# Row maxima of the attention scores by way of DRAM, two groups ahead, and another order of DVE work and loads in the first slot

## The chip, the cores and the metric

The kernel runs on one core of a Trainium2 chip. The metric is the device time of one launch in microseconds, the median of three runs. The engines are TensorE (PE; PEld is its weight load), VectorE (DVE), ScalarE (ACT), GpSimd (POOL) and SyncE (SP), whose queue starts nearly all transfers. Everything is float32.

## The reference

One pre-norm transformer layer, cut to what matters. There are 4 batches of 512 tokens, width 512, 32 query heads and 8 key heads of 16 dimensions, so 4 query heads share a key head; the feed-forward width is 1376.

```
x = resid                                   # (4, 512, 512)
n = layernorm(x)
q, k = rope(n @ Wq), rope(n @ Wk);  v = n @ Wv
att   = (q . k) / 4, causal                 # per query head, 512 x 512
probs = softmax(att)                        # needs the maximum of each row, or a bound of it
x = x + (probs @ v) @ Wo
n = layernorm(x)
x = x + (silu(n @ W_gate.T) * (n @ W_up.T)) @ W_down.T
```

## The kernel before, in words

The attention of a batch is worked in 8 groups of 4 heads. The 32 groups (`GROUPS`) are numbered through: group g belongs to batch g // 8. Four heads of a group stand in the four 32-row quarters of the partitions, and PE works with 32 rows at a time.

For each group the scores are made twice. The plain scores (`scores`, L436: queries on partitions, keys along the row) are only there to find the maximum of each row. `greatest` reads them: ACT copies heads 2 and 3 out of PSUM (L447), and DVE runs one masked minimum of the negated scores for each head and query tile (L454), first on heads 0 and 1 straight from PSUM, then on the copy. The negative maxima go to columns of the tile `low`. They are then needed along a row, not down a column: `lowered` has PE transpose the four 128 x 128 pieces of `low` (L471), and DVE adds the result to `qa` (L472). `qa` is the masked copy of a group's queries (`masked`, on POOL); in each quarter it has a row that `masked` leaves zero, and there the negative maxima come to stand. The keys carry a one at that place. So the second pass (`lowered_scores`, L480: keys on partitions, queries along the row) gives scores with the maximum already subtracted; ACT takes the exponential (L487), POOL clears the half above the diagonal (L491), and `averages` (L509) multiplies with the values. Their quotients are made later, from the queues `later` and `later_act`.

The four PSUM banks `sc` (two `pairs`) serve both passes in turn, for three rounds of query tiles (`rounds`), so each round of one pass waits until the round of the other has been read.

The order is written out by hand. `slot(b, steps)` runs the 8 groups of batch b. While it makes the lowered scores of group g, it makes the plain scores and maxima of group g + 1. Between these it places pieces of other matmul work: `gap` takes from `steps` what the shares in `shares` allow. Slot 0 gives the projections of batches 1 to 3; slots 1 to 3 give the output projection and the feed-forward of the batch before, and after slot 3 the last batch's follow alone. DVE work that may wait, such as the layer norms, stands in the queue `aside` and is taken by `do(aside)`.

A projection is made in two halves of matmuls (`halved`); its `finish` follows at once. For queries and keys that is `rotated`: DVE shuffles (L228) and multiplies (L230), POOL does the rest. `transposed` turns a normalised tile on PE (L195) and copies it out, the odd tiles on DVE (L198) and the even on ACT (L200). All of them take one of three PSUM banks from `bank`.

Weight loads (`load_w`, L158) and x loads stand on SP in the order of the program. Before slot 0 the kernel loads x of batch 0, all of wk, rope, wq, wv and wo, normalises and projects batch 0, and makes the plain scores of group 0; the norms and transposes of batch 1 are spread between its three rounds. Feed-forward weights are loaded by `load_f` two column blocks ahead.

Of the kernel before, what the change touches and what calls it, by code (L numbers as in the profile page):

```python
# [47 lines left out]
SWAP = [(d + 16) % 32 for d in range(32)]  # L48

# [25 lines left out]
def preln_block_kernel(  # L75
# [56 lines left out]


# [25 lines left out]

    def bank():  # L160
        return ps_mm.tile([P, T], F32, tag="mm", name="mm")
# [30 lines left out]
    def transposed(xn, i, xnT):  # L192
# [4 lines left out]
        if i % 2:  # L197
            nc.vector.tensor_copy(xnT[:, :, ts(i, P)], src)  # L198
        else:
            nc.scalar.copy(xnT[:, :, ts(i, P)], src)  # L200

    def halved(products, finish):
# [8 lines left out]
        def two():  # L211
            for step in products[len(products) // 2 :]:
                step(made["ps"])
            finish(made["ps"])
# [200 lines left out]
    def masked(g):  # L415
# [4 lines left out]
        qa[g] = work.tile([P, T], F32, tag="qa", name="qa", bufs=2)  # L420
# [19 lines left out]
    def greatest(g, at, lo, hi):  # L440
# [4 lines left out]
        hf = GROUPS[g][2]  # L445
        copy = work.tile([P, 2, T], F32, tag="copy", name="copy", bufs=2)
        nc.scalar.copy(copy[:, :, lo:hi], pairs[1][:, :, lo:hi])  # L447
        for pair, src in enumerate((pairs[0], copy)):
            for i, c in at:
                n = P * (i + 1)  # L450
                for r in range(2):
                    junk = work.tile([P, T], F32, tag="junk", name="junk")
                    row = 32 * (2 * pair + r) + 16 * (1 - hf)
# [8 lines left out]
                        accum_out=low[hf][:, i, row : row + 1],  # L462
                    )

    def lowered(g):
# [6 lines left out]
        nc.vector.tensor_tensor(qa[g], qa[g], pt, ALU.add)  # L472

# [70 lines left out]

    for i in range(NT):
        load_xr(0, i)
    load_w(wk_sb, wk)
    nc.sync.dma_start(out=rope_sb, in_=rope)
    load_w(wq_sb, wq)
    load_w(wv_sb, wv)  # L550
    load_w(wo_sb, wo)
# [7 lines left out]
    for t in low:  # L559
        nc.gpsimd.memset(t, 0.0)  # L560
    for n in range(4):
        nc.gpsimd.memset(values(n), 1.0)
    for cost, step in turned:
        step()
    begin1[1]()
    for cost, step in start[:4]:
# [6 lines left out]
    scores(0, rounds[0][0])  # L573
    greatest(0, *rounds[0])
    do(aside, 3)
    for cost, step in start[6:8]:
        step()
    scores(0, rounds[1][0])
    greatest(0, *rounds[1])
    do(aside, 2)  # L580
    for cost, step in (turned1[0], *start[8:10], turned1[1]):
        step()
    scores(0, rounds[2][0])
    greatest(0, *rounds[2])
    for cost, step in (*turned1[2:], *start[10:]):
        step()
    masked(1)
    lowered(0)

# [7 lines left out]
    def slot(b, steps):  # L597

        steps = deque(steps)
        total = sum(cost for cost, _ in steps)  # L600

        shares = [0.19, 0.17, 0.19, 0.2, 0.25]
        done, part, n = 0.0, 0.0, 0

        def gap():
            nonlocal done, part, n
            part += shares[n % 5]
            n += 1
            done = fill(steps, total * part / 8, done)

        for g in range(8 * b, 8 * b + 8):
# [3 lines left out]
            probabilities(((0, 0),), e0, T)  # L615
# [107 lines left out]
```

## Time and profile before

| | us |
|---|---|
| three timed runs | 989.32, 989.39, 993.88 |
| median | 989.39 |
| the profiled execution, whole | 993.68 |
| its span, first to last instruction | 992.0 |
| mean granted TensorE clock | 0.979 |
| first lowered scores of groups 0, 8, 16, 24 start at | 52.56, 225.31, 427.3, 635.0 |
| tail after the last slot, from about | 842 |

The span is what the engines' views divide; the profiled execution's own time is 1.7 us longer. Busy times overlap between engines and do not add up. A group of instructions has its line, engine, operation, and destination<-source; in the timeline each row begins with start and duration in us, and in brackets stands the idle time before it with what ended it. An answer by windows gives for each stretch its length and, engine by engine, the busy time and the number of instructions. PE and PEld overlap.

### The profile page before, as it was taken

To read this page: it belongs to the slowest core of one execution; us is meant where nothing else is said; L and a number is where in the kernel's file an instruction comes from. 1 tells how busy PE (TensorE), PEld (TensorE's weight loads), DVE (VectorE), ACT (ScalarE), POOL (GpSimd) and SP (SyncE) were. 2 spreads that over 40 slices of the span, in tenths; PEclk is the share of its full clock that TensorE was granted. 3 is DMA by queue.
4 is the path that set the end of the run, shared out by engine and by line. 5 is a ranking of instruction groups with operands and counts; after the bars stand their busy time and mean duration, and the time that the engine had idled before them with its cause. 6 is when DMAs were issued, how large, how long until landed. Compare 5 with 4: busy or idle time off the path is not lost.

```text
span 992.0 us, 12710 instructions
## 1 busy us (share of the span) xinstructions
PE 926.5 (93%) x4800; PEld 412.3 (42%) x4800; DVE 535.8 (54%) x1488; ACT 296.6 (30%) x385; POOL 216.0 (22%) x291
## 2 busy tenths in 40 slices
PE   6779887889899999999999999999999999999998
PEld 3334343443344444444444444444444443444443
DVE  5766677767665656475555564655655553312110
ACT  0134344443334333333333433323333431010000
POOL 5353354443311111212111111111111111100000
PEclk9898899999899999999999999999999999999999
DMA  6100100000244310040112110101212102022100
GB/s 212 43 1 1 34 11 1 2 1 1 65 159 126 84 45 26 11 170 11 53 45 53 43 50 11 54 1 43 54 43 54 41 19 64 11 75 75 47 11 32
DMA packets 56813, 46.63 MB, mean 47 GB/s; under 512 B 6352, under 2 KB 48336, under 8 KB 56496
## 3 DMA queue, kind: packets, MB, share of 16 engines
q1 hardware_dynamic: 56464, 40.05, 13.9%
q10 hardware_dynamic: 288, 5.77, 1.5%
q8 instruction: 38, 0.62, 0.3%
q14 instruction: 23, 0.19, 0.1%
HBM read 38.73 MB, written 7.08 MB: 46 GB/s over the span
## 4 chain that ended last, share of the span: by engine, by line
PE 77%; DVE 10%; ACT 5%; issue 2%; POOL 1%; DVEq 0%; ACTq 0%; POOLq 0%
PE mm L375 31%; PE mm L401 15%; PE sc L480 8%; PE av L509 8%; PE sc L436 7%; DVE junk L454 6%; PE mm L327 5%; ACT e L487 5%; PE mm L471 1%; PE mm L220 1%; DVE inv L532 1%; DVE st L175 0%; PE mm L195 0%; ACT xnT L200 0%; DVE inv L528 0%
## 5 line engine op out<-in xcount | busy, mean ns | idle before, releaser
L375 PE MATMUL mm<-xnT,shared 128*128 128x512 f32 (+1 forms) x704 | 324.2, 606 | 2.5 <-ACT xnT L200 2.5
L487 ACT ACTIVATE e<-sc 128x1024 f32<-128x1024 f32 (+1 forms) x192 | 160.6, 881 | 281.0 <-PE sc L480 268.0
L454 DVE CUSTOM_DVE_ANT_0 junk<-sc,mask 128x512 f32<-128x512 f32 (+3 forms) x256 | 125.6, 490 | 130.7 <-PE sc L436 94.1
L491 POOL TENSOR_SCALAR_AFFINE_SELECT e<-e 128x512 f32<-128x512 f32 x128 | 83.9, 667 | 512.8 <-issue 240.6
L375 PEld LDWEIGHTS mm<-xnT,shared 128*128 128x128 f32 (+1 forms) x704 | 126.2, 188 | 166.5 <-issue 159.0
L401 PE MATMUL mm<-wd_sb,home 128*128 128x512 f32 (+1 forms) x352 | 158.5, 599 | 0.0
L454 DVE CUSTOM_DVE_ANT_0 junk<-copy,mask 128x512 f32<-128x512 f32 (+3 forms) x256 | 131.2, 513 | 19.7 <-DVE low L454 0.5
L447 ACT COPY copy<-sc 128x1024 f32<-128x1024 f32 (+1 forms) x96 | 83.6, 871 | 194.7 <-PE sc L436 172.0
L480 PE MATMUL sc<-qa,home 32*128 32x512 f32 (+3 forms) x1024 | 96.3, 468 | 12.4 <-DVE low L454 10.2
L436 PE MATMUL sc<-home,qa 32*128 32x512 f32 (+3 forms) x1024 | 94.3, 460 | 10.7 <-ACT e L487 10.0
L401 PEld LDWEIGHTS mm<-wd_sb,home 128*128 128x128 f32 (+1 forms) x352 | 64.9, 190 | 82.7 <-issue 81.6
L509 PE MATMUL av<-e,home 128*32 128x512 f32 (+3 forms) x1024 | 80.7, 459 | 0.0
L480 PEld LDWEIGHTS sc<-qa,home 32*128 32x128 f32 x1024 | 43.3, 184 | 81.6 <-DVE low L454 54.3
L384 DVE SCALAR_TENSOR_TENSOR g<-g,mm 128x512 f32<-128x512 f32 (+1 forms) x44 | 30.2, 686 | 86.5 <-ACT g L383 86.5
L436 PEld LDWEIGHTS sc<-home,qa 32*128 32x128 f32 x1024 | 47.2, 187 | 64.8 <-issue 21.0
L327 PE MATMUL mm<-wo_sb,cx 128*128 128x512 f32 x128 | 62.0, 623 | 5.7 <-POOL cx L533 5.7
L220 PE MATMUL mm<-xnT,shared 128*128 128x512 f32 x120 | 62.2, 655 | 1.7 <-DVE xnT L198 0.9
L386 DVE TENSOR_TENSOR home<-mm,g 128x512 f32<-128x512 f32 (+1 forms) x44 | 30.4, 690 | 52.8 <-PE mm L375 52.7
L383 ACT ACTIVATE g<-mm 128x512 f32<-128x512 f32 (+1 forms) x44 | 26.3, 598 | 100.9 <-PE mm L375 100.9
L532 DVE RECIPROCAL inv<-inv 128x256 f32<-128x256 f32 x32 | 55.3, 1739 | 0.1
L405 DVE SCALAR_TENSOR_TENSOR xr<-mm,xr 128x512 f32<-128x512 f32 x16 | 11.0, 690 | 78.7 <-PE mm L401 78.7
L509 PEld LDWEIGHTS av<-e,home 128*32 128x32 f32 x1024 | 30.0, 114 | 40.2 <-issue 37.6
(70 smaller groups left out, 561.3 us busy)
## 6 DMA issues: line engine op xcount, KB each, us to landing
shared<-in_wg SPq DMA_DIRECT2D x40, 256.0 KB, 2.8
shared<-in_wu SPq DMA_DIRECT2D x40, 256.0 KB, 2.9
xr<-in_x SPq DMA_DIRECT2D x16, 256.0 KB, 3.5
out<-xr SPq DMA_DIRECT2D x16, 256.0 KB, 2.0
xa<-in_x SPq DMA_DIRECT2D x12, 256.0 KB, 2.8
spill<-wd_sb ACTq DMA_DIRECT2D x1, 2816.0 KB, 9.0
home<-spill ACTq DMA_DIRECT2D x1, 2816.0 KB, 12.5
wd_sb<-in_wd SPq DMA_DIRECT2D x1, 2560.0 KB, 10.8
```

The costliest lines, as they stand in the source:

```text
L220: nc.tensor.matmul(ps, lhsT=w[:, k, ts(m, P)], rhs=xnT[:, k, :], start=k == 0, stop=k == NK - 1)
L327: nc.tensor.matmul(ps, lhsT=cx[m][:, ts(i, P)], rhs=wo_sb[:, m, :], start=m == 0, stop=m == 3)
L375: nc.tensor.matmul(ps[:m, :], lhsT=wgu[c][:, a, k, :m], rhs=xnTs[""][:, k, :], start=k == 0, stop=k == NK - 1)
L401: nc.tensor.matmul(py[i], lhsT=homes[n][:m, f, ts(i, P)], rhs=wd_sb[:m, f, :], start=f == 0, stop=f == NF - 1)
L436: nc.tensor.matmul(sc[r][:, c : c + n], lhsT=qa[g][rows, ts(i, P)], rhs=k[rows, :n], start=True, stop=True)
L447: nc.scalar.copy(copy[:, :, lo:hi], pairs[1][:, :, lo:hi])
L454: nc.vector.tensor_tensor_reduce(out=junk[:, :n], in0=src[:, r, c : c + n], in1=mask[:, T - n :], scale=-1.0, scalar=BIG, op0=ALU.add, op1 ...
L480: nc.tensor.matmul(sc[r][:, c : c + T - P * j], lhsT=k[rows, ts(j, P)], rhs=qa[g][rows, P * j :], start=True, stop=True)
L487: nc.scalar.activation(e[:, 2 * n : 2 * n + 2, :], pairs[n][:, :, :width], AF.Exp, scale=1.0 / math.sqrt(DH))
L491: nc.gpsimd.affine_select(out=e[:, :, c : c + P], in_=e[:, :, c : c + P], compare_op=ALU.is_ge, fill=0.0, base=0, pattern=[[0, 4], [1, P]] ...
L509: nc.tensor.matmul(av[32 * r : 32 * r + 32, P * j :], lhsT=v[:, j, 4 * (m // 2) + r, DH * (1 - hf) : DH * (3 - hf)], rhs=e[:, r, c : c + n ...
L532: nc.vector.reciprocal(r, r)
```

## The change

Three things are done.

Groups from `NEAR` = 9 on no longer use `lowered`. Their negative maxima go to a small tile `packed` (128 x 32, one column for each head and query tile). `turned_round` transposes it on DVE in blocks of 32 x 32 and stores it to DRAM (`lowest`). `laid_out` loads it from there with four transfers straight into the zero row of `qa`, each 4 x 4 pieces of 32 numbers. All five are issued on SP.

For these groups the plain scores are made two groups ahead (`h = g + 2`), `masked` runs one group earlier and `qa` has three buffers. Group 8 makes the plain scores of both group 9 and group 10, with extra gaps between them. In `gap`, shares are given by each call.

Up to the end of slot 0 (`thin`) the order differs. x of batch 1 and the first 128 columns of wq are loaded ahead of wv, the rest of wq and wo; the norms of batch 1 are made right after the first half of batch 0's key matmuls are issued, and its transposes and keys follow the third round of group 0's plain scores. Odd transposed tiles are also copied by ACT. A projection's `finish` is put off into the queue `full`, taken in `greatest` between and after the two sets of maxima (or by `bank`, if more than one is waiting). `averages(g)` stands ahead of `lowered(h)`, with a gap after it (the former also holds in later slots, where `lowered` is not called for the next group). `do(aside)` is called at other places.

```diff
@@ -130,6 +132,10 @@
     low = [const.tile([P, NT, P], F32, name=f"low{hf}") for hf in range(2)]
 
 
+    packed = [const.tile([P, 32], F32, name=f"packed{n}") for n in range(3)]
+    lowest = [dram.tile([P, 32], F32, name=f"lowest{n}") for n in range(2)]
+
+
 
     homes = [const.tile([P, NF, T], F32, name=f"home{n}") for n in range(3)] + [wd_sb]
     spill = dram.tile([P, NF, T], F32, name="spill")
@@ -157,7 +163,13 @@
     def load_w(t, src):
         nc.sync.dma_start(out=t, in_=src.rearrange("(k p) m -> p k m", p=P))
 
+
+    full = deque()
+    thin = [True]
+
     def bank():
+        while len(full) > 1:
+            full.popleft()()
         return ps_mm.tile([P, T], F32, tag="mm", name="mm")
 
 
@@ -194,7 +206,7 @@
         for k in range(NK):
             nc.tensor.transpose(pt[:, ts(k, P)], xn[:, ts(k, P)], ident)
         src = pt.rearrange("p (k q) -> p k q", k=NK)
-        if i % 2:
+        if i % 2 and not thin[0]:
             nc.vector.tensor_copy(xnT[:, :, ts(i, P)], src)
         else:
             nc.scalar.copy(xnT[:, :, ts(i, P)], src)
@@ -211,7 +223,10 @@
         def two():
             for step in products[len(products) // 2 :]:
                 step(made["ps"])
-            finish(made["ps"])
+            if thin[0]:
+                full.append(lambda: finish(made["ps"]))
+            else:
+                finish(made["ps"])
 
         return one, two
 
@@ -417,7 +432,7 @@
         if g >= len(GROUPS):
             return
         b, m, hf = GROUPS[g]
-        qa[g] = work.tile([P, T], F32, tag="qa", name="qa", bufs=2)
+        qa[g] = work.tile([P, T], F32, tag="qa", name="qa", bufs=3)
         nc.gpsimd.tensor_scalar(qa[g], homes[HOME[b]][:, m, :], halves[hf], 1.0, ALU.mult, ALU.mult)
 
     def keys_of(g):
@@ -443,14 +458,20 @@
         if g >= len(GROUPS):
             return
         hf = GROUPS[g][2]
+
+        def found(head, i):
+            if g < NEAR:
+                row = 32 * head + 16 * (1 - hf)
+                return low[hf][:, i, row : row + 1]
+            return packed[g % 3][:, NT * head + i : NT * head + i + 1]
+
         copy = work.tile([P, 2, T], F32, tag="copy", name="copy", bufs=2)
         nc.scalar.copy(copy[:, :, lo:hi], pairs[1][:, :, lo:hi])
-        for pair, src in enumerate((pairs[0], copy)):
+        def maxima(pair, src):
             for i, c in at:
                 n = P * (i + 1)
                 for r in range(2):
                     junk = work.tile([P, T], F32, tag="junk", name="junk")
-                    row = 32 * (2 * pair + r) + 16 * (1 - hf)
                     nc.vector.tensor_tensor_reduce(
                         out=junk[:, :n],
                         in0=src[:, r, c : c + n],
@@ -459,8 +480,14 @@
                         scalar=BIG,
                         op0=ALU.add,
                         op1=ALU.min,
-                        accum_out=low[hf][:, i, row : row + 1],
+                        accum_out=found(2 * pair + r, i),
                     )
+
+        maxima(0, pairs[0])
+        if lo == 0:
+            do(full, len(full))
+        maxima(1, copy)
+        do(full, len(full))
 
     def lowered(g):
 
@@ -470,6 +497,22 @@
         for i in range(NT):
             nc.tensor.transpose(pt[:, ts(i, P)], low[GROUPS[g][2]][:, i, :], ident)
         nc.vector.tensor_tensor(qa[g], qa[g], pt, ALU.add)
+
+    def turned_round(g):
+        if g >= len(GROUPS):
+            return
+        t = small.tile([P, 32], F32, tag="turned", name="turned", bufs=2)
+        nc.vector.transpose(t, packed[g % 3])
+        nc.sync.dma_start(out=lowest[g % 2], in_=t)
+
+    def laid_out(g):
+
+        if g >= len(GROUPS):
+            return
+        rows = qa[g].rearrange("(r s) (i a q) -> r s i a q", r=4, i=NT, a=4)[:, 16 * (1 - GROUPS[g][2])]
+        src = lowest[g % 2].rearrange("(a u r i) q -> u i r a q", a=4, u=2, r=4)[0]
+        for i in range(NT):
+            nc.sync.dma_start(out=rows[:, i], in_=src[i])
 
     def lowered_scores(g, at):
 
@@ -542,13 +585,14 @@
     HOME = {0: 0, 1: 1, 2: 2, 3: 1}
 
 
+    def load_columns(t, src, lo, hi):
+        nc.sync.dma_start(out=t[:, :, lo:hi], in_=src[:, lo:hi].rearrange("(k p) m -> p k m", p=P))
+
     for i in range(NT):
         load_xr(0, i)
     load_w(wk_sb, wk)
     nc.sync.dma_start(out=rope_sb, in_=rope)
-    load_w(wq_sb, wq)
-    load_w(wv_sb, wv)
-    load_w(wo_sb, wo)
+    load_columns(wq_sb, wq, 0, P)
 
     (begin1, turned1, rest1), (begin2, turned2, rest2), (begin3, turned3, rest3) = (
         projections(b, b) for b in range(1, B)
@@ -556,36 +600,38 @@
     begin, turned, start = projections(0, 0, early=True)
     begin[1]()
     do(aside, len(aside))
-    for t in low:
+    begin1[1]()
+    load_w(wv_sb, wv)
+    load_columns(wq_sb, wq, P, D)
+    load_w(wo_sb, wo)
+    for t in (*low, *packed):
         nc.gpsimd.memset(t, 0.0)
-    for n in range(4):
-        nc.gpsimd.memset(values(n), 1.0)
+    nc.gpsimd.memset(values(0), 1.0)
+    thin[0] = False
     for cost, step in turned:
         step()
-    begin1[1]()
-    for cost, step in start[:4]:
+    for cost, step in start[:1]:
+        step()
+    do(aside, len(aside))
+    for n in range(1, 4):
+        nc.gpsimd.memset(values(n), 1.0)
+    for cost, step in start[1:4]:
         step()
     masked(0)
     for cost, step in start[4:6]:
         step()
 
     rounds = (((3, 0),), 0, T), (((2, 0), (0, 3 * P)), 0, T), (((1, 2 * P),), 2 * P, T)
-    scores(0, rounds[0][0])
-    greatest(0, *rounds[0])
-    do(aside, 3)
-    for cost, step in start[6:8]:
-        step()
-    scores(0, rounds[1][0])
-    greatest(0, *rounds[1])
-    do(aside, 2)
-    for cost, step in (turned1[0], *start[8:10], turned1[1]):
-        step()
-    scores(0, rounds[2][0])
-    greatest(0, *rounds[2])
-    for cost, step in (*turned1[2:], *start[10:]):
-        step()
+    thin[0] = True
+    for at, steps in zip(rounds, ([*start[6:8]], [*start[8:10]], [*turned1, *rest1[:2]])):
+        scores(0, at[0])
+        greatest(0, *at)
+        for cost, step in steps:
+            step()
     masked(1)
     lowered(0)
+    for cost, step in start[10:]:
+        step()
 
     def fill(steps, upto, done):
         while steps and done + steps[0][0] / 2 <= upto:
@@ -598,48 +644,76 @@
 
         steps = deque(steps)
         total = sum(cost for cost, _ in steps)
-
-        shares = [0.19, 0.17, 0.19, 0.2, 0.25]
-        done, part, n = 0.0, 0.0, 0
-
-        def gap():
-            nonlocal done, part, n
-            part += shares[n % 5]
-            n += 1
-            done = fill(steps, total * part / 8, done)
-
-        for g in range(8 * b, 8 * b + 8):
+        done, part = 0.0, 0.0
+        groups = range(8 * b, 8 * b + 8)
+        shares = 8 + 0.5 * (NEAR - 1 in groups)
+        thin[0] = b == 0
+
+        def gap(share):
+            nonlocal done, part
+            part += share / shares
+            done = fill(steps, total * part, done)
+
+        for g in groups:
+            h = g + 1 if g + 1 < NEAR else g + 2
             if g % 8 == 7:
                 do(aside, len(aside))
             lowered_scores(g, ((0, 0),))
             probabilities(((0, 0),), e0, T)
+            if g + 1 > NEAR:
+                laid_out(g + 1)
             do(later)
+            if not thin[0]:
+                do(aside)
+            gap(0.17 if thin[0] else 0.19)
+            if h == NEAR + 1:
+                for at, lo, hi in rounds:
+                    scores(NEAR, at)
+                    greatest(NEAR, at, lo, hi)
+                    gap(0.17)
+                turned_round(NEAR)
+                laid_out(NEAR)
+            at, lo, hi = rounds[0]
+            scores(h, at)
+            greatest(h, at, lo, hi)
             do(aside)
-            gap()
-            at, lo, hi = rounds[0]
-            scores(g + 1, at)
-            greatest(g + 1, at, lo, hi)
-            do(aside)
-            gap()
+            gap(0.15 if thin[0] else 0.17)
             lowered_scores(g, ((1, 0), (3, 3 * P)))
             probabilities(((1, 0), (3, 3 * P)), e1, T)
             do(later_act)
             do(later)
-            do(aside)
-            gap()
+            if not thin[0]:
+                do(aside)
+            gap(0.17 if thin[0] else 0.19)
             at, lo, hi = rounds[1]
-            scores(g + 1, at)
-            greatest(g + 1, at, lo, hi)
-            gap()
+            scores(h, at)
+            greatest(h, at, lo, hi)
+            if thin[0]:
+                do(aside)
+            gap(0.17 if thin[0] else 0.2)
             at, lo, hi = rounds[2]
             lowered_scores(g, ((2, 0),))
-            scores(g + 1, at)
-            greatest(g + 1, at, lo, hi)
+            scores(h, at)
+            greatest(h, at, lo, hi)
+            if h > NEAR:
+                turned_round(h)
             probabilities(((2, 0),), e2, 2 * P)
-            masked(g + 2)
-            gap()
-            lowered(g + 1)
+            if h == NEAR - 1:
+                masked(NEAR)
+                masked(NEAR + 1)
+            elif h < NEAR:
+                masked(g + 2)
+            else:
+                masked(g + 3)
+            gap(0.17 if thin[0] else 0.25)
             averages(g)
+            if h < NEAR:
+                lowered(h)
+            if thin[0]:
+                do(aside)
+                gap(0.17)
+        thin[0] = False
+        do(full, len(full))
         for cost, step in steps:
             step()
         do(later, len(later))
@@ -658,7 +732,7 @@
     def restored():
         nc.scalar.dma_start(out=homes[1], in_=spill)
 
-    slot(0, [begin2, *rest1, *turned2, begin3, *rest2, *turned3, *rest3[:-4]])
+    slot(0, [begin2, *rest1[2:], *turned2, begin3, *rest2, *turned3, *rest3[:-4]])
 
     before, behind = attended(0)
     tiles = list(down(0, 0))
```

More of the change, by code (lines that the diff above doesn't have):

```diff
@@ L48 @@
 SWAP = [(d + 16) % 32 for d in range(32)]
+NEAR = 9
 GROUPS = [(b, m, hf) for b in range(B) for m in range(4) for hf in range(2)]
```

## The prediction

> **What bounds the kernel now.** I read the page's busy table and its forty slices first, to see whether one engine is full and where it is not.
>
> ```profile
> PE 926.5 (93%) x4800; PEld 412.3 (42%) x4800; DVE 535.8 (54%) x1488; ACT 296.6 (30%) x385; POOL 216.0 (22%) x291
> PE   6779887889899999999999999999999999999998
> PEclk9898899999899999999999999999999999999999
> ```
>
> TensorE carries the kernel. Each slice is 24.8 us. From the eleventh on PE is at nine tenths; the first ten are holed, and the dips of the granted clock lie mostly there. The share of 93% is thus a mean over two regimes. To separate them I asked for the engines' busy time slot by slot, cutting where the first lowered scores (L480) of groups 0, 8, 16 and 24 start in the timeline; each row gives start and end, length, then busy time.
>
> ```profile
> 52.56:225.31 172.75, 143.64 (x1033) 68.67 (x1033) 121.56 (x363) 68.81 (x87) 80.61 (x95) 0.94 0.03 7
> 225.31:427.30 201.99, 195.38 (x1099) 84.67 (x1096) 121.97 (x344) 73.26 (x95) 40.57 (x57) 0.98 0.22 67
> 427.30:635.00 207.70, 203.97 (x1113) 88.11 (x1112) 117.35 (x337) 71.72 (x94) 33.63 (x52) 0.99 0.18 54
> 635.00:842.00 207.00, 201.48 (x1076) 86.94 (x1075) 113.03 (x308) 68.21 (x89) 33.82 (x52) 1.00 0.14 40
> ```
>
> In slots 1 to 3 PE has 600.8 of 616.7 us: any PE work taken out shortens them. In slot 0 PE idles 29 us, while DVE is busy for 121.6 of 172.75; there the handing to and fro of the score banks sets the time. The timeline of PE shows both regimes at the place of the edit, first in slot 0, then in slot 1.
>
> ```profile
> 138.34 0.27 PE L471 MATMUL mm<-ident,low 128*128 128x128 f32 x1
> 139.84 0.55 PE L471 MATMUL mm<-ident,low 128*128 128x128 f32 x3 [1.23 <-DVE low L454]
> 140.31 2.36 PE L509 MATMUL av<-e,home 128*32 128x512 f32 x32
> ...
> 349.74 0.60 PE L471 MATMUL mm<-ident,low 128*128 128x128 f32 x4
> 350.27 2.36 PE L509 MATMUL av<-e,home 128*32 128x512 f32 x32
> ```
>
> In slot 0 PE waits for the last maxima before it transposes them, with 2.3 us of independent averages queued behind that wait. In slot 1 nothing waits. Then PE's waits inside slot 0, in us and times:
>
> ```profile
> PE sc L480 <- DVE low L454: 10.0, 7, 2.0
> PE sc L436 <- ACT e L487: 7.9, 14, 2.1
> PE mm L471 <- DVE low L454: 7.3, 6, 1.8
> PE sc L480 <- DVE qa L472: 1.5, 1, 1.5
> PE mm L471 <- ACT xnT L200: 1.5, 2, 1.3
> ```
>
> And the start, in the timeline of PE:
>
> ```profile
> 41.79 0.63 PE L195 MATMUL mm<-ident,xa 128*128 128x128 f32 x4 [2.89 <-DVE xa L183]
> 43.90 1.11 PE L195 MATMUL mm<-ident,xa 128*128 128x128 f32 x4 [1.49 <-DVE home L230]
> 44.81 5.76 PE L220 MATMUL mm<-xnT,shared 128*128 128x512 f32 x8
> 52.56 1.14 PE L480 MATMUL sc<-qa,home 32*128 32x512 f32 x8 [1.55 <-DVE qa L472]
> ```
>
> Here PE waits on the norms of batch 1, and eight matmuls that take 3.70 us elsewhere take 5.76: the clock was at half after the gaps.
>
> **Part 1, slots 1 to 3: maxima through DRAM.** Groups 9 to 31, 23 of them, lose the four transposes of L471. Their place on PE is the step from 349.74 to 350.27: 0.53 us (the 281 ns mean of one counts overlapped latency; four would be 1.1 us). 23 x 0.53 = 12.2 us, all on the path, since PE has no other work to wait for there. At 0.60, the row's own length, it would be 13.8; if half went back into the 15.9 us of idle already there, 6.
>
> In their place come, per group, a DVE transpose of 128x32, one store and four loads. DVE loses the add of L472 (0.68 us). No row has a DVE transpose; it lies between the 128x1 accumulator read (0.08) and the 128x512 shuffle (0.73), so DVE loses nothing, or gains up to 0.6 us, off the path. The DMAs stand on SP: four loads of xr were issued in 1.80 us, so five cost some 2.25 us there. A store to DRAM landed in 2.0 us (out, 256 KB), a load in 2.8 (wg): 2.0 + 2.8 + 2.25 = 7 us by the nearest rows; by the farthest, 9.0 (spill) + 12.5 (its return) + 2.25 = 24 us. In the timeline the last maxima of the next group end at 349.1; with scores two groups ahead the lowered scores that need the result come a whole group later, at 377.37. 28 us cover either price, so I take nothing. Behind SP's new waits stand only weight loads, x loads and output stores: a weight load is issued two column blocks ahead (about 13.8 us of PE work for 2.8 us of landing), and hidden too. Without the cover the price would be PE waiting 22 times.
>
> "DMA: Bandwidth & Descriptors" of the Trainium skill, under its rules for kernel authors, says that transfers under 64 KB are mostly overhead and should be coalesced; its fit charges about 2 us fixed each. These carry 16 KB and 2 KB. An estimate from that page, five one after the other, is 10 us, still under the cover; the rule speaks against the change but decides nothing unless landings queue.
>
> Group 8 now scores two groups; the step shares give it 1.5 parts, and a gap of 0.17 parts holds 2.3 us of matmuls, more than the 1.45 us of two 512-wide maxima. I cost it at nothing; a miss would be some 2 us. The plain scores' zero row, the third qa buffer and the earlier copy of the mask move work of equal size.
>
> **Part 2, the start.** The norms of batch 1 (four times about 1.0 of statistics and 0.55 of scaling, 6.2 us) leave the stretch from 28 to 43 us, where DVE is full, for the hole from 12.7 to 19.3, where DVE waits 6.62 us for the first keys. x of batch 1 is queued on SP ahead of wv, most of wq and wo; it still waits for its buffers until 12 us, and behind that the other three weights now wait: 2 MB at the 370 GB/s seen there, 6 us, done by 19; the values need theirs at 22.5, the next queries at 28. Three memsets on Pool (4.3 us) move to 18.7, so keys are spread 0.8 us later. Then, going through the rounds of group 0 with the rows' lengths: scores at 27.7, second round at 32.4, third at 37.1, four transposes and batch 1's keys to 44.3, maxima lowered to 44.9, queries (3.6 us) over the add, first lowered scores at 48.5 instead of 52.56. That is 4 us; from a loss of 1 (the Pool delay and nothing else) to a gain of 7 (the half clock gone too).
>
> **Part 3, slot 0.** It takes 21.6 us a group.
> - Averages ahead of the lowering: the 7.3 + 1.5 us of waits at L471 go under the 2.3 us of averages. What is late next is the add with its hand-over, about 1.0 us a group, which was hidden; a step now follows, but four steps a group are spread over six gaps, so some 4 us of 8 come back. Gain 5.
> - Finishes held back until pair 0 is read, and odd copies on ACT: the shuffle and product (0.73 + 0.67) no longer stand ahead of the maxima that free the banks. Of the 10.0 us of L480 waiting for maxima most is the two maxima themselves (1.45 us). Gain 4, between 0 and 10. Waits for ACT's exponentials (7.9) stay. The norms now stand behind the second round and can push the third: up to -0.8 a group, inside that bound.
> - The keys of batch 1 (3.4 us of PE) have left the slot, but mostly fill holes: 1.
> - Half clock: four matmuls at 63.35 take 3.40 us against 1.98, averages at 72.46 take 3.97 against 2.36, and so on; five such places cost 8.4 us. They follow idles of 1.7 to 2.1 us (62.04: 2.06; 71.99: 1.70). Gaps near 2 us will remain, at the exponentials: gain 1.5, between 0 and 8.4.
>
> Sum 11.5 us (20.1 us a group), from 0 to 24.
>
> "TensorE: Matmul & The Clock Gate", section on what is actually happening, puts the throttle after an idle window of about 3.4 us. By it none of these gaps should have cost anything; the five places contradict it. Were the gate as it says, and the present dips chance, the gain might take all 8.4 and the sum be 35 instead of 28.
>
> **Sum.** 12.2 + 4 + 11.5 = 27.7 us. The profiled execution took 993.68 us (span 992.0), which makes 966. The three timed runs have their median at 989.39, 4.3 less, so I predict 962. About 0.5%, 5 us, is what a measurement of this kernel tells from no change.
>
> **Rivals.**
> - Only Part 1 works: DVE's rounds in slot 0 are as slow as before because the same 9.4 us of maxima a group still gate the banks, and the start's gain is eaten by the Pool delay. For it: most waits in slot 0 are for the maxima or exponentials themselves. 989.4 - 12.2 = 977; with half given back, 983. Chance 0.22.
> - Slot 0 loses nearly all holes: demand at full clock is 8 x 8.2 (scores, lowered scores, averages, lowering) + 56 of steps = 122 us on PE, 119 on DVE. At 18.7 us a group the slot gives 23, the start 6: 989.4 - 41 = 948. Against it: the chain of scores, exponentials, maxima through four banks comes to about 19 us by its rows. Chance 0.12.
> - Slower: DRAM round trips land behind the lowered scores, since SP's queue is held (SP already waits 307 us in all for output stores) and each laid-out load stands behind such a wait. It decides once chain and queue exceed 28 us; to outweigh 28 us of gain, PE must lose 1.3 us at each of 22 groups. At 2 us, with the half clock that follows such gaps (1.5), 22 x 3.5 = 77: 1038. Against it: every wait on SP is for work that PE has passed by then. Chance 0.08.
> - The change nets nothing: Part 1 half given back and slot 0 slower by as much, 986 to 994. Chance 0.04.
>
> **How the numbers follow.** The forecast keeps 0.54. The range, 945 to 980, takes in the first two rivals and the bounds of parts 2 and 3; it leaves out the slower half of the first and the last two. Faster by over 0.5%: 0.54 + 0.12 + 0.22 less a tail of 0.01, 0.87; same 0.05; slower 0.08.
>
> **What would show it.** The profile after should have 36 transposes of low instead of 128, PE at full share in slots 1 to 3 with some 4 us less each, first lowered scores near 48.5, slot 0 near 161 us, no wait of L480's successor on a DMA. Wrong would be: PE waits for DMA in slots 1 to 3, slot 0 over 172, or the first f block waiting for weights.

## The result and the profile after

The changed kernel takes 1022.84 us (median of four runs, 1021.18 to 1023.58) against 989.36 for the kernel before in the same job: a ratio of 1.033, 95% interval 1.031 to 1.0345. The prediction was 962, with 0.08 for slower. Its profiled execution took 1022.58 us, span 1020.6, mean granted clock 0.962 (before 0.979).

The page's busy table and two rows of its forty slices, of the kernel after (a slice is now 25.5 us):

```profile
PE 928.0 (91%) x4708; PEld 407.2 (40%) x4708; DVE 537.4 (53%) x1482; ACT 299.7 (29%) x391; POOL 218.7 (21%) x294
PE   6867777777889999998999999999999999999998
PEclk9988888887999999999999999999999999999999
```

PE has lost the 92 transposes and is busy no less: slices three to ten show 8 or 7 tenths of the clock. The windows by slot, cut at the first lowered scores (now L523) of groups 0, 8, 16, 24 and at the end of slot 3 (start and end, length, busy time of PE, PEld, DVE, ACT, POOL, then granted clock, DMA share, GB/s):

```profile
51.15:259.27 208.12, 152.42 (x1025) 75.33 (x1025) 128.90 (x356) 70.95 (x91) 83.08 (x93) 0.85 0.02 6
259.27:459.72 200.45, 192.51 (x1085) 79.90 (x1084) 126.68 (x376) 74.80 (x96) 41.47 (x58) 0.99 0.22 66
459.72:667.78 208.06, 200.58 (x1085) 84.53 (x1081) 113.63 (x336) 71.78 (x93) 33.62 (x52) 0.99 0.17 53
667.78:865.20 197.42, 194.38 (x1021) 81.43 (x1017) 97.58 (x270) 66.75 (x87) 31.58 (x49) 0.99 0.15 41
```

The later cuts given for the kernel before, in its table and in the prediction (427.3, 635.0), were some 2 us late: the first lowered scores of groups 16 and 24 start at 424.94 and 632.69 there. With these, in us:

| | before | after | |
|---|---|---|---|
| start | 52.56 | 51.15 | -1.4 |
| slot 0 | 172.75 | 208.12 | +35.4 |
| slots 1 to 3 and the tail | 766.69 | 761.33 | -5.4 |

So the whole loss, and more, is in slot 0. PE's waits there in the kernel after (us in total, times, longest):

```profile
PE av L552 <- POOL e L534: 37.8, 8, 6.4
PE sc L523 <- DVE low L475: 13.6, 10, 1.6
PE sc L451 <- ACT e L530: 2.9, 10, 0.6
```

The waits at the transposes of `low` (7.3 us before) are gone and those for ACT's exponentials nearly so. In their place PE stands eight times, once a group, at the last quarter of the averages. The timeline of the kernel after, all engines, shows what that is (start, duration):

```profile
149.96 0.60 ACT L530 ACTIVATE e<-sc 128x512 f32<-128x512 f32 x1 [2.08 <-DVE low L475]
...
150.89 0.72 DVE L243 STREAM_SHUFFLE rot<-mm 128x512 f32<-128x512 f32 x1
...
151.69 1.26 POOL L244 TENSOR_TENSOR rot<-rot,rope_sb 128x512 f32<-128x512 f32 x1 [2.17 <-DVE rot L243]
153.03 1.26 POOL L246 TENSOR_TENSOR home<-home,rot 128x512 f32<-128x512 f32 x1
154.25 0.64 POOL L534 TENSOR_SCALAR_AFFINE_SELECT e<-e 128x512 f32<-128x512 f32 x1
...
154.94 1.08 PE L552 MATMUL av<-e,home 128*32 128x256 f32 x8 [6.43 <-POOL e L534]
```

The exponential of the third round ends at 150.56. POOL could clear it at once, but a put-off finish stands ahead of it in POOL's queue: its product with the sine waits for DVE's shuffle, its sum follows, and the clearing comes 3.7 us late.

### The profile page after: what moved, and what is told of

It reads as the page before. It is cut to its first block, busy times and chain, and to the rows that moved or that the text cites. A ratio compares the mean times of both kernels' runs of the same rounds, so it can differ in the third digit from the quotient of the medians.

```text
span 1020.6 us, 12774 instructions
## 1 busy us (share of the span) xinstructions
PE 928.0 (91%) x4708; PEld 407.2 (40%) x4708; DVE 537.4 (53%) x1482; ACT 299.7 (29%) x391; POOL 218.7 (21%) x294
## 4 chain that ended last, share of the span: by engine, by line
PE 77%; DVE 10%; ACT 5%; issue 3%; POOL 3%; DMA 1%; SPq 0%; ACTq 0%; DVEq 0%; POOLq 0%
PE mm L390 30%; PE mm L416 14%; PE sc L523 8%; PE sc L451 7%; PE av L552 6%; DVE junk L475 5%; ACT e L530 5%; PE mm L235 5%; PE mm L342 4%; DMA xr<-in_x 1%; PE mm L498 1%; PE mm L290 1%; PE mm L207 1%; DVE st L187 1%; POOL e L534 1%
## 5 line engine op out<-in xcount | busy, mean ns | idle before, releaser
L475 DVE CUSTOM_DVE_ANT_0 junk<-copy,mask 128x512 f32<-128x512 f32 (+3 forms) x256 | 146.0, 570 | 18.3 <-ACT home L299 0.5
L523 PE MATMUL sc<-qa,home 32*128 32x512 f32 (+3 forms) x1024 | 101.3, 490 | 17.9 <-DVE low L475 13.6
L523 PEld LDWEIGHTS sc<-qa,home 32*128 32x128 f32 x1024 | 45.9, 195 | 91.8 <-DVE packed L475 35.0
L235 PE MATMUL mm<-xnT,shared 128*128 128x512 f32 x120 | 66.8, 696 | 0.8 <-issue 0.8
```

Source lines behind the costliest of these rows:

```text
L235: nc.tensor.matmul(ps, lhsT=w[:, k, ts(m, P)], rhs=xnT[:, k, :], start=k == 0, stop=k == NK - 1)
L475: nc.vector.tensor_tensor_reduce(out=junk[:, :n], in0=src[:, r, c : c + n], in1=mask[:, T - n :], scale=-1.0, scalar=BIG, op0=ALU.add, op1 ...
L523: nc.tensor.matmul(sc[r][:, c : c + T - P * j], lhsT=k[rows, ts(j, P)], rhs=qa[g][rows, P * j :], start=True, stop=True)
```

## The experiments

The times are medians of four executions, where no other number is given; where a range matters it is given. The kernel before had medians of 989.4 to 990.4 beside these runs. Ratios are to it, with 95% intervals.

### The two halves of the change

**DRAM alone.** The old start and slot 0, with the way through DRAM from group 9 on.

> The route through DRAM with scores two groups ahead from group 9 on, with the loads, the start and the first slot of the kernel before. If the route is worth what the changed kernel's later slots show against before (slot 1 +0.8, slot 2 +0.3, slot 3 -4.6, tail -1.9): 984 us. If it is worth the forecast 12.2 and the changed first slot spoils the later ones: 977. If the route itself costs: above 990.

985.73 us, ratio 0.9957 (0.9942 to 0.9972): a gain, but a third of the 12.2 predicted.

**Order alone.** The changed start and slot 0 without DRAM: `NEAR = 40`, and `lowered` ahead of `averages` again from slot 1 on.

> The loads, the start and the first slot of the changed kernel, without the route through DRAM (all groups lowered by PE, in the later slots ahead of the averages, as before). If the loss is the first slot's alone (+35.4) less the start's gain (1.4): 1023 us, plus what the route gained: 1023 to 1029. If part of the loss comes from the route: below 1018.

1026.37, 1.0373 (1.0358 to 1.0389). The loss is in the order; the DRAM half takes 3.8 us off the kernel before and 3.5 off this one.

### Inside the changed slot 0

**Clearing first.** Put-off finishes of the third round go behind the exponentials and the clearing of `e2`; only POOL's order changes:

```diff
         maxima(1, copy)
-        do(full, len(full))
+        if lo == 0 or not in_slot[0]:
+            do(full, len(full))
...
             probabilities(((2, 0),), e2, 2 * P)
+            do(full, len(full))
```

> Only the order on POOL differs from the changed kernel: in the first slot the put-off finishes of the third round are issued after the clearing of e2, not before it. POOL theory (the averages wait because the two rope operations of a finish, 1.27 us each and themselves waiting for a DVE shuffle, stand ahead of the clearing of e2): the second exponential of e2 ends near 150.56 in the trace of the changed kernel and the clearing starts at 154.25, so about 3.6 us go in each of 8 groups, 29 us, and with them part of the half clock that follows; 985 to 997 us. Cover theory (averages simply stand too early on PE, with no matmul step ahead of them, whatever POOL does): the wait moves to the exponential, at most 10 us are gained; 1012 to 1022.

1010.31, 1.0206 (1.0189 to 1.0222). POOL's queue was worth 12.5 of the 33 us. That lies between the two forecasts, and averages still waited 26.9 us for the clearing, so this order is one part only:

```profile
PE av L554 <- POOL e L536: 26.9, 8, 5.8
```

**Averages last.** `lowered(h)` ahead of `averages(g)` again:

> Only the order on PE differs from the changed kernel: in the first slot the lowering stands ahead of the averages again, as before the change. POOL theory: the averages still wait for the clearing of e2, and only the lowering (1.1 us at half clock) and the add move under that wait; 1 to 2 us a group, 1007 to 1015 us. Cover theory: the order on PE is the cause, so most of the 35 us lost in the first slot come back; 985 to 997.

1022.9, 1.0336 (1.0319 to 1.0354): nothing, outside both forecasts. The wait only moves; PE's waits in slot 0 of this kernel begin with

```profile
PE mm L498 <- DVE low L475: 36.5, 16, 4.5
```

The third round is late on DVE as much as on POOL, whichever product asks for it first.

**A step ahead, spare products, and both parts.** First, the fourth step of a group ahead of the averages (`gap(0.25)` there and `gap(0.09)` behind, for 0.17 and 0.17):

> Only the order on PE differs from the changed kernel: two shares of the first slot are 0.25 and 0.09 in place of 0.17 and 0.17, so the fourth step of a group stands ahead of the averages (where PE waits 37.8 us in 8 groups) and no longer behind the lowering. Step theory (a step of 1.98 us, 2.7 to 3.6 at half clock, was taken out of the hole ahead of the averages and put where nothing is waited for): 8 times 2 to 3.5 us, less about 1 us each for the add that is uncovered now; 1000 to 1012 us. POOL theory alone: the averages start when POOL has cleared e2, and what follows is shorter by the step; the same sum without the clock, 1010 to 1015. If the place of the step does not matter: 1021 to 1024.

1020.68, 1.0304 (1.0286 to 1.0323). Then two spare products (four matmul instructions) ahead of the averages of each group, their result unused:

> The changed kernel with work added: in each group of the first slot two spare products (4 matmul instructions, 1.9 us at full clock, read by nobody) stand ahead of the averages. Clock theory (61 us of the first slot are at half clock because PE idles some 5 us ahead of the averages; PE busy there would keep the clock): the added work fits into the hole and costs nothing, and a part of the 25 to 30 us lost to the clock comes back; 1000 to 1015 us. If the clock follows something else, or the hole is only moved: 1022 to 1030.

1019.6, 1.0293 (1.0272 to 1.0314). In slot 0 the granted clock rose from 0.85 to 0.93, though PE had more work, and the slot was only 3 us shorter. The half clock thus looks like a consequence here, since PE waits for DVE and POOL at any clock; but the test is not a clean one, because in two places the spare products themselves waited for copies on ACT, 7.4 us in all. Last, clearing first together with the step ahead:

> The changed kernel with both: the clearing of e2 ahead of the put-off finishes on POOL, and the fourth step ahead of the averages on PE. If the two causes add up: 1010 less 15 to 20, 990 to 995 us. If one hole takes the place of the other: within 5 us of the better of the two alone. If nothing else is wrong in the first slot: 172 us there, 983.

1007.94, 1.017 (1.0151 to 1.019): 2.4 better than clearing first alone. None of these brings back more than 3.3 us.

### POOL beside DVE

A second thing stood in the timeline of the kernel after: the minima on the SBUF copy take twice their time beside POOL.

```profile
138.20 0.68 DVE L245 TENSOR_TENSOR kr<-mm,rope_sb 128x512 f32<-128x512 f32 x1
138.38 1.27 POOL L244 TENSOR_TENSOR rot<-rot,rope_sb 128x512 f32<-128x512 f32 x1 [2.18 <-DVE rot L243]
...
138.79 1.41 DVE L475 CUSTOM_DVE_ANT_0 junk<-copy,mask 128x512 f32<-128x512 f32 x1
...
139.73 1.59 POOL L246 TENSOR_TENSOR kr<-kr,rot 128x512 f32<-128x512 f32 x1
...
140.24 1.63 DVE L475 CUSTOM_DVE_ANT_0 junk<-copy,mask 128x512 f32<-128x512 f32 x1
```

Alone such a minimum takes 0.69 and the POOL operation 1.27. Each minimum ends some 0.55 us behind the end of the POOL operation. Counted over slot 0 of the kernel after, the 512-wide minima on the copy average 1.52 us where they overlap a product or sum of POOL's (10) and 0.69 where they overlap nothing (6); 384-wide, 1.36 (8) and 0.56 (7). Minima straight from PSUM keep 0.69 beside POOL. In the kernel before two of the 384-wide and none of the 512-wide overlap: there `finish` ran ahead of the maxima; the change puts it between the two sets.

**No sine.** Clearing first, with POOL's two rope operations left out of the put-off finishes in slot 0 (the queries and keys of batches 1 to 3 lack that part):

> This is the kernel of the first experiment (finishes of the third round behind the clearing of e2; 1010.3 us), but POOL's two operations of every put-off rope finish in slot 0 (the product with the sine and the sum) are left out, so queries and keys of batches 1 to 3 lack that part of the rotation; PE, DVE and ACT do the same work. Theory of the shared port: DVE's minima on the SBUF copy take 1.36 to 1.52 us beside such a POOL operation and 0.56 to 0.69 alone; without it no group has a minimum over 1 us, DVE's busy time in slot 0 falls by some 12 to 15 us, and the time to 995 to 1000. Theory that only the order of DVE's and POOL's queues counts (the length of the minima being beside the path): 1006 to 1011.

994.92, 1.0058 (1.0041 to 1.0074).

**Fills in their place.** The same two operations replaced by fills of about their length, which read nothing:

```diff
+        def busy():
+            for n in (T, T, P):
+                nc.gpsimd.memset(rot[:, :n], 0.0)
...
-        engine.tensor_tensor(rot, rot, sin, ALU.mult)
+        if put_off: busy()
+        else: engine.tensor_tensor(rot, rot, sin, ALU.mult)
```

(and likewise for the sum).

> The kernel of the first experiment (1010.3 us) with POOL's two operations of each put-off rope finish in slot 0 replaced by fills of about the same length (memsets of 512, 512 and 128 columns, 1.2 us together by the rows of the mask and of low), so POOL is as busy as before but reads nothing; queries and keys of batches 1 to 3 lack that part of the rotation. Left out altogether, the two operations gave 994.9. Theory of the shared port (DVE's minima on the copy are stretched by POOL reading SBUF): no minimum over 1 us, 994 to 999. Theory of POOL's load (clearing and finishing late because POOL is busy): minima short or not, 1006 to 1011.

998.12, 1.0092 (1.006 to 1.0124). The groups of the 512-wide minima on the copy, of the kernel after and of this one (over the whole execution; busy us, mean ns of one, then idle time ahead):

```profile
L475 DVE CUSTOM_DVE_ANT_0 junk<-copy,mask 128x512 f32<-128x512 f32 x64 | 52.6, 822 | 5.3 <-ACT home L299 0.5
```

```profile
L488 DVE CUSTOM_DVE_ANT_0 junk<-copy,mask 128x512 f32<-128x512 f32 x64 | 44.2, 691 | 5.7 <-ACT home L312 0.5 <-DVE packed L488 0.5
```

POOL is nearly as busy in slot 0 (79.1 us, 83.7 with clearing first), ten such minima still run beside it, none over 0.69. So of the 15.4 us that leaving the operations out returns, 12.2 are POOL's reading and 3.2 its being busy, each uncertain by some 2 us, since the four executions spread from 995.8 to 1001.3. The forecast by the theory of the shared port, 994 to 999, came true.

**Finishes behind both sets.** Clearing first, and nothing taken from `full` between the two sets of maxima; nothing is left out:

```diff
         maxima(0, pairs[0])
-        if lo == 0:
-            do(full, len(full))
         maxima(1, copy)
```

> The kernel of the first experiment (1010.3 us), with the put-off finishes taken only behind both sets of maxima, no longer between them. Nothing is left out. Theory of the shared port: POOL's part then lies beside the next round's maxima from PSUM or beside nothing, the number of long minima on the copy falls from 15 or more to a few, and the time to 997 to 1003. Theory that the finishes cost by standing in DVE's queue at all: 1008 to 1014.

1005.44, 1.0168 (1.0152 to 1.0183). One 512-wide and two 256-wide minima on the copy still run beside a product or sum of POOL's (0.86, 1.46 and 0.45 us), yet only 5 us come back. That lies between the two forecasts: with less contention the later finish seems still to cost, which no run separates further.

**Finishes at once.** The changed kernel without `full` (`if False:` for `if thin[0]:` in `halved`):

> The changed kernel (1022.8 us) with every projection finished at once, as before the change; shares of the steps, places of the norms, copies on ACT and averages ahead of the lowering stay as changed. If putting the finishes off carries most of slot 0's loss (shared port, POOL's clearing behind two rope operations, a later first step): 995 to 1003. If the places of the norms and the fourth step behind the lowering carry it: 1014 to 1022.

1003.15, 1.0147 (1.0127 to 1.0168). Putting off carries 19.7 of the 33 us.

### One piece at a time on the better half

**x loads first.** In the kernel with DRAM alone, the x loads of slot 2 stand behind the laid-out loads, as in the kernel after. There, on the queues of SP and ACT and on DVE:

```profile
460.98 1.95 SPq L180 DMA_DIRECT2D xr<-in_x  x4
461.10 0.34 ACTq L733 DMA_DIRECT2D home<-spill  x1
470.57 0.69 DVE L345 TENSOR_TENSOR xr<-mm,xr 128x512 f32<-128x512 f32 x1 [5.04 <-DMA xr<-in_x]
```

The loads are issued 1.3 us into the slot (1.5 ahead of it in the kernel before), beside the return of the 2.8 MB spill. DVE waits 5.04 us for them, the maxima of that round queue behind its add, and the next lowered scores start after 3.76 us of idle. The edit issues them ahead:

```diff
     before, behind = attended(1)
+    before.pop(0)[1]()
```

> The run with the DRAM route alone, but the four x loads of slot 2 are issued on SP ahead of the four loads of laid-out maxima. SP theory (the x loads stood 2.7 us later than before, behind those loads, and so behind the restore of 2.8 MB; PE lost 3.8 us to the wait and some 2 to the clock): 985.7 less 5 to 6, 980 us. If the wait comes from the restore alone: unchanged, 985 to 986.

982.07, 0.9912 (0.9888 to 0.9936), and no such wait: slot 2 takes 204.28, against 208.20 with DRAM alone and 208.06 in the kernel after. The four executions took 979.3 to 984.1. This kernel is the base of the next five.

**Averages ahead, alone.** `averages(g)` ahead of `lowered(h)`:

> The best kernel so far (982.1 us: old start and slot 0, way through DRAM, x loads first) with only the averages ahead of the lowering in slots 0 and 1. The prediction's step took 5 us for this: 977. Theory that the averages themselves wait for POOL's clearing at that place, and that the add with its hand-over is then uncovered: 981 to 987.

976.17, 0.9864 (0.9848 to 0.9879), 13 us faster than the kernel before and the fastest measured.

**Finishes put off, alone:**

> The same best kernel (982.1 us) with only the finishes of projections put off in slot 0 (taken between and behind the two sets of maxima, as in the change). The prediction's step took up to 4 us of gain from this: 978 to 980. Theory of the shared port and of POOL's clearing behind the put-off rope operations: minima on the copy of 1.3 to 1.5 us return, and the time rises by 12 to 20: 994 to 1002.

999.53, 1.0106 (1.0085 to 1.0128): +17.5 us. Twenty-two wide minima are stretched (1.54 and 1.39 on average), and DVE's busy time in slot 0 is 135.2 us against the base's 121.6.

**Norms moved, alone:**

> The same best kernel (982.1 us) with only the norms taken at the changed places in slot 0: behind the second round's maxima and behind the averages, not ahead of rounds. The prediction allowed up to 0.8 us a group against it. Theory that the norm ahead of the third round's maxima delays exponentials and the lowering: 985 to 990. Theory that the norms are beside the path: 981 to 983.

991.41 (ten executions, 985.3 to 992.1), 1.0012 (0.9996 to 1.0027): +9.3 us. PE's waits at the transposes of `low` go from 6.5 to 11.9 us in slot 0: a norm (0.69, 0.18, 0.15 and 0.54 us on DVE, as at 147.56 in the kernel after) stands ahead of the third round's minima.

**Copies on ACT, alone:**

> The best kernel of the third set's base (982.1 us: old start and slot 0, way through DRAM, x loads first) with only the odd transposed tiles of slot 0 copied by ACT instead of DVE. The prediction's step counted this together with the put-off finishes as a gain of 4; finishes put off cost 17.5 alone. If the DVE time that is freed shortens the rounds: 979 to 981. If the copy, standing behind an exponential that waits for maxima, holds a bank and PE's next transposes: 984 to 988.

985.83 (ten executions, 982.0 to 989.2), 0.9963 (0.9944 to 0.9982): +3.8 us by the medians, with ranges that overlap. In the profiled execution, the fastest, slot 0 takes 172.55 us, and 172.59 in the base's; where the loss of the other executions lies is not shown.

**The new start, alone.** The changed start, then the old slot 0 (`thin[0] = False`, `lowered` first), DRAM and x loads first:

> Slot 0 in the order of before, slots 1 to 3 with the way through DRAM and the x loads ahead of the laid-out loads (982.1 us with the old start), and the start as changed, up to the first lowered scores of group 0. The start alone was 1.4 us shorter in the changed kernel, and the keys of batch 1 and two more steps have left slot 0: 978 to 981. If the new start leaves a delay behind in slot 0 (later values, the masked queries, clock): 982 to 988.

985.43 (ten executions, 979.9 to 987.7), 0.9951 (0.9937 to 0.9966): 3.4 more than with the old start, again with ranges that overlap. Group 0's lowered scores start at 51.34 against 51.47; slot 0 then takes 175.88 against 172.59.

**The change mended.** The changed kernel with finishes at once, norms at the old places and x loads first:

> The changed kernel (1022.8 us) with three edits: finishes at once, norms at the old places in slot 0, x loads of slot 2 ahead of the laid-out loads. Kept are the way through DRAM, the new start, odd copies on ACT, averages ahead of the lowering and the step behind them. If the single prices add up (base 982.1, averages -5.9, new start +3.3, copies near nothing): 978 to 982. If pieces that were not tried alone (the other shares, the step behind the lowering) cost: 984 to 990.

995.12 (five executions, 983.0 to 995.3), 1.0057 (1.004 to 1.0074). With the copies' 3.8, the single prices sum to 982.1 - 5.9 + 3.4 + 3.8 = 983.4. Some 12 us are missing by the median. But the five executions took 983.0, 990.1 and three times about 995, at mean granted clocks of 0.989, 0.980 and 0.974: the fastest meets the sum, so part of the 12 us goes with the clock of the execution. Another part is waiting: in the profiled one (990.1) PE idles 37.9 us in slot 0, 9.4 more than in "averages ahead, alone". Going the other way, 982.1 - 5.9 + 17.5 + 9.3 + 3.8 + 3.4 + 3.7 (x loads) = 1013.9, 9 less than the changed kernel. By the medians a piece not tried alone, such as the shares with their sixth gap, or the meeting of the pieces, costs about 10. Here PE's first wait in slot 0 is

```profile
PE av L552 <- POOL e L534: 18.1, 8, 3.1
```

and in "averages ahead, alone" it is

```profile
PE av L552 <- POOL e L534: 1.7, 3, 0.7
```

There a step fills the time of exponential and clearing; with the change's sixth gap the group's fourth step falls behind the lowering, and the averages stand bare. That is where it is; moving that step in the changed kernel gave only 2.2 and 2.4 us, so as a cause it is argued, not shown.

## Why the prediction was wrong

**The step that failed** is Part 3, slot 0: predicted -11.5 us, measured +35.4. Its terms:

- **Finishes held back and odd copies on ACT: "Gain 4, between 0 and 10".** Measured alone, +17.5 and +3.8 (the second hardly clear of the scatter): the wrong sign, and outside its bounds. The step counted the 0.73 and 0.67 us that leave DVE's path and not the two POOL operations issued with them. These now run beside the minima on the copy and stretch them, and in the third round they stand ahead of the clearing that the averages need. POOL's queue was passed over, though half the finish is on it. The trace of before already showed the price: two 384-wide minima there overlap POOL's product or sum and take 1.28 us, not 0.56.
- **Norms: "up to -0.8 a group, inside that bound".** Measured +9.3 us, 1.2 a group, and not inside.
- **Averages ahead of the lowering: "Gain 5".** Measured alone, 5.9: right in size, but by luck, as the rows below show. In the changed slot it gave nothing, since the next wait, for DVE's and POOL's third round, was longer than the averages. Nor was the mechanism the one priced. These are the slot 0 rows of the base and of "averages ahead, alone":

```profile
51.47:224.06 172.59, 145.78 (x1032) 70.05 (x1033) 121.60 (x363) 68.76 (x87) 80.59 (x95) 0.93 0.03 7
```

```profile
52.26:219.06 166.80, 138.32 (x1032) 66.58 (x1033) 121.34 (x364) 68.86 (x87) 80.44 (x95) 0.98 0.03 7
```

PE's idle time rose by 1.7 us (26.81 to 28.48, length less busy), with the add's hand-over at 0.9 a group as foreseen. Its busy time fell by 7.5 for the same work, at a clock of 0.98 instead of 0.93. The "half clock" term, put at 1.5 (0 to 8.4), was the whole gain.

**Part 1, 12.2 us.** Sign right, two terms off. With x loads first, PE's busy time from slot 1 on falls from 746.15 to 736.72 and its idle time stays (20.5, 20.2): 9.4 us or 0.41 a group, all on the path, where 0.53 was taken. (The medians show 7.3 to 8.3, or 0.32 to 0.36 a group; the profiled execution of before was 4.3 over its median.) The other is "behind SP's new waits stand only weight loads, x loads and output stores ... hidden too": not the x loads of slot 2, 3.7 us. The round trip itself was hidden as claimed; no lowered scores waited for a landing. SP waited 20.8 us in all for stores to land, 2.6 at most, before the laid-out loads. The rival of late round trips did not come true; slower came true by another way, which no rival named.

**Part 2, 4 us.** Measured 1.4. Over the kernels with the new start, group 0's lowered scores start between 49.5 and 52.6, with the old one between 50.9 and 52.6, so even this is within their scatter, and slot 0 gave back 3.3 behind it. The hole at the norms did close, and the eight matmuls that took 5.76 us take 3.70, as the timeline of PE in the kernel after shows:

```profile
43.64 3.70 PE L235 MATMUL mm<-wd_sb,shared 128*128 128x512 f32 x8 [0.68 <-ACT wd_sb L212]
...
51.15 1.14 PE L523 MATMUL sc<-qa,home 32*128 32x512 f32 x8
```

Though 2.9 us of wait and 2.1 of matmul time went, group 0's lowered scores start only 1.4 us earlier. The rest was lost ahead of these rows. The kernel after and then "finishes at once", which has the same order up to the first plain scores, show it:

```profile
18.31 2.69 POOL L617 MEMSET home<- 128x1536 f32 x2
18.39 2.88 DVE L195 TENSOR_SCALAR xa<-xa,mv,rstd 128x512 f32<-128x512 f32 x1 [0.44 <-POOL rstd L190]
21.20 0.73 DVE L243 STREAM_SHUFFLE rot<-mm 128x512 f32<-128x512 f32 x1
...
28.78 2.00 PE L451 MATMUL sc<-home,qa 32*128 32x512 f32 x8 [2.45 <-POOL qa L436]
30.71 4.49 PE L235 MATMUL mm<-xnT,shared 128*128 128x512 f32 x8
```

```profile
28.91 1.14 PE L451 MATMUL sc<-home,qa 32*128 32x512 f32 x8 [3.24 <-POOL qa L436]
29.98 3.70 PE L235 MATMUL mm<-xnT,shared 128*128 128x512 f32 x8
```

The last norm's scaling, moved beside the fills that were moved too, takes 2.88 us instead of 0.54, as in all 13 kernels with the new start. The shuffle of the first keys then starts at 21.20, not 19.31, and the first plain scores at 28.78, where 27.7 was forecast: the term "keys are spread 0.8 us later" was 1.9. Behind that wait the kernel after ran at half clock and lost another 1.7 us; "finishes at once" did not, and its lowered scores start at 49.46.

The second rival's demand on PE was too low as well: 122 us were taken for slot 0 at full clock, and "averages ahead, alone" is busy for 138.32 at a clock of 0.98.

"SBUF — State Buffer" of the Trainium skill, section "Who interferes with whom", states what the prediction should have looked up: a DVE instruction with two SBUF inputs contends with a GpSimd instruction that reads SBUF, not with one that only writes it, and one with at most one SBUF input does not contend, outside the modes in which DVE uses both of its port pairs. For the minima this case agrees on each: 1.52 us for copy and mask beside a POOL product, 0.69 beside a POOL fill, 0.69 for PSUM and mask beside a product. Whether the scaling that took 2.88 us beside fills ran in such a mode, no run here shows.

## What to carry to other kernels

When a piece of work is put off, follow every instruction it issues to its own queue, and ask what it will run beside: here putting off 1.4 us of DVE's work a finish brought 17.5 us back, through POOL. Test each piece of a bundled change alone on the best base: one of five gained 5.9 us and was hidden under the losses of the others. When loads are put on a queue with others, look at the one whose due time is nearest, not at the typical one.

## What the runs showed of the hardware

DVE's minima and POOL slow each other by operand place, not by load: about 0.8 us for each wide minimum on the copy beside a product or sum of POOL's, whose own time goes from 1.27 to as much as 1.60. The later one waits: in the kernel after, four 256-wide minima that start 0.1 us ahead of a clearing keep their 0.42 us, and the clearing takes 0.83 instead of 0.64. A fill is not harmless to everything on DVE: beside fills the scaling of a norm, from SBUF to SBUF, took 2.88 us instead of 0.54.

The clock after a gap is not decided by the gap's length alone. The same products after the same idle time, first in the base, then in "averages ahead, alone":

```profile
150.44 2.09 PE L451 MATMUL sc<-home,qa 32*128 32x384 f32 x16 [2.12 <-ACT e L530]
152.46 3.78 PE L235 MATMUL mm<-xnT,shared 128*128 128x512 f32 x4
```

```profile
145.73 1.15 PE L451 MATMUL sc<-home,qa 32*128 32x384 f32 x16 [2.12 <-ACT e L530]
146.81 1.98 PE L235 MATMUL mm<-xnT,shared 128*128 128x512 f32 x4
```

2.12 us of idle cost 2.7 us more in the one and nothing in the other. At the start a longer wait even kept the clock, as shown above: 3.24 us at full clock behind it, 2.45 us at half. One program differs so from run to run: the mended kernel took 983.0 us at a mean granted clock of 0.989 and 995.2 at 0.974. "TensorE: Matmul & The Clock Gate", section "What's actually happening", calls the activity window free-running, so that where the work lies in it counts; that fits, but no run here moved the work against the window.
